# A neighbour mask turned by VectorE instead of TensorE in a two-layer graph network

## The chip, the cores and the metric

One core of a Trainium2 chip runs the whole kernel. The metric is device time in microseconds (us) for one execution, the median of several. TensorE is the matrix engine, VectorE (DVE in the profile) and ScalarE (ACT) do elementwise work, GpSimd (POOL) does elementwise work and issues transfers, SyncE (SP) issues transfers. SBUF is the on-chip memory with 128 partitions, PSUM the memory into which TensorE writes[...].

## What is computed

128 graphs of 128 nodes with 256 features each pass through two layers. The change is in layer 0, in its message passing between neighbours:

```python
h = jnp.maximum(_layernorm(x, axis=-1), 0.0)
s = h @ w_se.T + b_se                          # three features for each node
sq = jnp.sum(s * s, axis=-1)
dist = sq[:, :, None] + sq[:, None, :] - 2.0 * jnp.einsum('bnd,bmd->bnm', s, s)
A = jnp.exp(-dist) * mask                      # mask is adj, (128, 128, 128) of 0 and 1
msg = jax.nn.relu(h @ w_msg.T + b_msg)
x_nmp = jnp.einsum('bnm,bmd->bnd', A, msg)
```

The other parts of layer 0 are two convolutions along the nodes (one of width 17, computed here by a Fourier transform) and a gated unit which takes the convolution's result, `x_nmp` and `h`. Layer 1 works on 25 nodes of each graph alone. All data are float32.

## The kernel before

Graphs are worked on in 32 groups of four (`GB = 4`, `NQ = 32`). Four stages follow one another on TensorE. `stage_a(q)` normalizes a group, turns it, stores it transposed in DRAM (`hTd[q]`), and applies the first convolution and the Fourier transform. `stage_b(bat)` multiplies the 40 frequencies of half of all graphs. Both run twice, for groups 0 to 15 and for 16 to 31: a, b, a, b. Then `stage_c(q)` does the gated unit, and `block(blk)` the second layer beside it.

The message passing is in `early(q)`, once for each group, and runs beside the stages as a filler. Its body is the generator `neighbours` (L608 to L660). The loads for it are issued one group ahead by `load_n(q)` (L571): the transposed features `hT` (512 KB) and the adjacency `ad` (256 KB), both on SyncE's queue, into buffers of which there are two each. The queue also carries stage_b's weights (`wf`, L512) and stage_a's input (`xa`, L381), in program order.

`neighbours` computes, in this order, with a `yield` after each step:

1. `pse` (L614), the node features, and `ef` and `lr`, the factors of the distance (L618, L621);
2. the messages for two graphs and then for the other two: `pm` (L630), evacuated to `msg` by VectorE (L633) and ScalarE (L635);
3. the attention: `pds[j]` (L643) gets the exponent of graph j; `adj` of graph j is transposed by TensorE into the other half of the same PSUM tile (L645); ScalarE takes the exponential into `aT[:, j]` (L647); VectorE multiplies `aT[:, j]` by the transposed adjacency out of PSUM (L648);
4. twice: `px` (L656), messages by attention, for two graphs, evacuated to `xnmp` (L658).

The attention is needed with the sending node on the partitions, which is why the adjacency has to be turned.

The order of all instructions is fixed when the program is built. Each generator yields two numbers: the time that its step takes on TensorE, and a delay before which its next step isn't due. `Order.run` (L183) keeps a clock, takes of the lanes whose next step is due the one with the least work done in proportion to its weight, and lets it emit its next step. The engines then run their instruction streams in that order, each in its own, waiting on semaphores. Lane `beside` holds `early`; its weight is 0.66 and 0.2 beside the two runs of stage_a, 0.5 and 0.65 beside those of stage_b, and 0.5 afterwards.

In stage_b one frequency is a product `pa` of two factors and a product `pb` of their sums (L526). GpSimd forms the sums in SBUF one frequency ahead (`xs`, L520, and the third slot of `wf`, L521). ScalarE copies `pb` to `kk` (L557), and VectorE forms `y` from `pa` and `kk` (L558), which GpSimd's queue stores (L562). During the second stage_a GpSimd also folds the gate weights (`fold_gates`, L326).

PSUM is divided into three buffers `gat` and five buffers `tmp`, a bank each; `pds` takes four of `tmp` and each is free again after the last reader of it. The pool `fr`, which holds `ef`, `lr`, `msg`, `aT`, has one buffer for each name.

Of the kernel before, what the change touches and what calls it, by code (L numbers as in the profile page):

```python
# [9 lines left out]
FP = mybir.dt.float32  # L10
AF = mybir.ActivationFunctionType
# [4 lines left out]
B, N, D = 128, 128, 256  # L16
# [3 lines left out]
P = 128  # L20
GB = 4
# [20 lines left out]
WIDE = 32  # L42
# [165 lines left out]
def kernel(ctx: ExitStack, tc: tile.TileContext, x, adj, consts, vecs, w_se, conv1_w,  # L208
                    conv2_w, w_msg, b_msg, w_ih, w_hh, W1, W2, b2, fusion_w, out):
    nc = tc.nc  # L210
# [7 lines left out]
    ptmp = ctx.enter_context(tc.tile_pool(name="ptmp", bufs=5, space=PSUM))  # L218
# [14 lines left out]
    def c(name):  # L233
        a, b = CAT[name]
        return cst[:, a:b]
# [5 lines left out]
    ident = c("ident")  # L241
# [127 lines left out]
    LATE, XA, MOM = {}, {}, {}  # L369
# [201 lines left out]
    def load_n(q):  # L571
        hT = LATE["io"].tile([P, 2, 512], FP, tag="hT", name=f"hT{q}")
        nc.sync.dma_start(out=hT, in_=hTd[q])
        ad = LATE["io"].tile([P, GB, N], FP, tag="adj", name=f"adj{q}")
        nc.sync.dma_start(out=ad, in_=adj[q * GB:(q + 1) * GB].rearrange("b n m -> n b m"))
        return hT, ad

    SUMS = {}
# [29 lines left out]
    def neighbours(q, hT, ad, xm):  # L608


        pse = ptmp.tile([P, 512], FP, tag="tmp", name=f"pse{q}")
        for k in range(2):
            for j in range(GB):
                nc.tensor.matmul(pse[j * WIDE:(j + 1) * WIDE, :N], wse9[:, k],  # L614
                                 hT[:, k, j * N:(j + 1) * N], start=(k == 0), stop=(k == 1))
        ef = LATE["fr"].tile([P, 4, N], FP, tag="ef", name=f"ef{q}")
        for i in range(4):
            nc.scalar.activation(ef[:, i], pse[:, :N], AF.Identity, scale=emb[:, i:i + 1],  # L618
                                 bias=embb[:, i:i + 1])
        lr = LATE["fr"].tile([P, 2, N], FP, tag="lr", name=f"lr{q}")  # L620
        nc.vector.tensor_tensor(lr, ef[:, 0::2], ef[:, 1::2], ALU.mult)  # L621
        yield 0.5, 0.0

        msgs = []
        for h in range(2):
            pm = ptmp.tile([P, 2, D], FP, tag="tmp", name=f"pm{q}_{h}")
            for i in range(2):
                j = 2 * h + i
                for k in range(2):
                    nc.tensor.matmul(pm[:, i], hT[:, k, j * N:(j + 1) * N], LATE["wmsg"][:, k],  # L630
                                     start=(k == 0), stop=(k == 1))
            msg = LATE["fr"].tile([P, 2, D], FP, tag=f"msg{h}", name=f"msg{q}_{h}")
            nc.vector.tensor_tensor(  # L633
                msg, pm, LATE["bmsg"][:, None, :].to_broadcast([P, 2, D]), ALU.add)
            nc.scalar.activation(msg, msg, AF.Relu)  # L635
            msgs.append(msg)
            yield 1.75, 0.0

        pds = [ptmp.tile([P, 2, N], FP, tag="tmp", name=f"pd{q}_{j}") for j in range(GB)]
        aT = LATE["fr"].tile([P, GB, N], FP, tag="aT", name=f"aT{q}")  # L640
        for j in range(GB):
            rows = slice(j * WIDE, (j + 1) * WIDE)
            nc.tensor.matmul(pds[j][:, 0], lr[rows, 0], lr[rows, 1], start=True, stop=True)  # L643
        for j in range(GB):
            nc.tensor.transpose(pds[j][:, 1], ad[:, j], ident)  # L645
        for j in range(GB):
            nc.scalar.activation(aT[:, j], pds[j][:, 0], AF.Exp)  # L647
            nc.vector.tensor_mul(aT[:, j], aT[:, j], pds[j][:, 1])  # L648
        yield 0.9, 3.0


        for h in range(2):
            px = ptmp.tile([P, 2, 2, N], FP, tag="tmp", name=f"px{q}_{h}")
            for i in range(2):
                for dc in range(2):
                    nc.tensor.matmul(px[:, dc, i], msgs[h][:, i, dc * P:(dc + 1) * P],  # L656
                                     aT[:, 2 * h + i], start=True, stop=True)
            nc.vector.tensor_copy(xm[:, :, h * 256:(h + 1) * 256],  # L658
                                  px.rearrange("p d i n -> p d (i n)"))
            yield 0.9, 0.0  # L660

    def early(q):

        while q not in A_DONE:
            yield 0.0, 0.5
        if q not in EN:
            EN[q] = load_n(q)
            yield 0.0, 6.0
        hT, ad = EN.pop(q)
        if q + 1 < NQ and q + 1 in A_DONE:  # L670
            EN[q + 1] = load_n(q + 1)
        xm = LATE["fr"].tile([P, 2, 512], FP, tag="xnmp", name=f"xnmp{q}", bufs=2)
        yield from neighbours(q, hT, ad, xm)
        nc.gpsimd.dma_start(out=xmd[q], in_=xm)
        E_DONE.add(q)
# [510 lines left out]
```

## Time and profile before

| | us |
|---|---|
| median of 3 runs | 2072.65 |
| lowest and highest of them | 2071.14, 2078.92 |
| span of the profiled execution | 2070.6 |
| TensorE busy (share of the span) | 2032.3 (98%) |
| VectorE busy | 1161.9 (56%) |
| GpSimd busy | 730.1 (35%) |
| ScalarE busy | 712.7 (34%) |

The span runs from the first instruction of the program to the last one in the profiled execution; the times of the runs also hold what lies around it. The granted TensorE clock was 0.993 over the span. By 40 slices of 51.8 us, the 16 DMA engines are busy for more than nine tenths up to 155 us (stage_a), for 0.74 to 0.90 of the time from 155 to 362 us (the first stage_b and the end of what lies before it), for 0.48 to 0.60 from 362 to 518 us, for 0.77 or 0.78 up to 673 us (the second stage_b), and for less than half of the time after that.

In the views below PE is TensorE's matmul, PEld its weight load, which overlaps it; a line such as L645 is the line of the kernel; `pd<-cst,adj` names what is written and read. TensorE's matmuls overlap each other as well, so that what one costs is read from the start of one group to the start of the next.

### The profile page before, as it was taken

The numbers are of one execution on the slowest core, as the hardware profiler recorded it, in microseconds if no ns is written. First come the engines' busy times: TensorE is split into PE (matmuls) and PEld (weight loads), VectorE is DVE, ScalarE is ACT, GpSimd is POOL, SyncE is SP. The second block draws the span as 40 slices with busy tenths as digits, with TensorE's granted clock in tenths as the row PEclk, the third lists the DMA queues.
The fourth block names the chain that finished last, engine by engine and source line by source line (L and its number), as shares of the span: only waits on it lengthen the run. The fifth ranks groups of instructions, "written<-read, shape, count | busy, mean of one in ns | idle before, by whom it ended". The sixth has DMA issues, their size and how long they took to land.

```text
span 2070.6 us, 31082 instructions
## 1 busy us (share of the span) xinstructions
PE 2032.3 (98%) x11316; PEld 1649.4 (80%) x11316; DVE 1161.9 (56%) x2711; ACT 712.7 (34%) x1611; POOL 730.1 (35%) x898
## 2 busy tenths in 40 slices
PE   7998999999999999999999999999999999999998
PEld 5667888888888788788778787878787888778875
DVE  6774445874433556646654654566456655654542
ACT  4663223444222444233222332232332323323333
POOL 3552665333664123322422243233223323233230
PEclk9999999999999999899999999999999999999999
DMA  9997788545777444223323232322232332323121
GB/s 215 294 284 237 259 273 269 180 153 202 254 257 249 142 125 139 75 75 90 85 62 90 84 83 76 106 79 75 82 93 72 81 96 80 86 77 102 35 74 52
DMA packets 190135, 281.72 MB, mean 136 GB/s; under 512 B 23625, under 2 KB 143374, under 8 KB 189982
## 3 DMA queue, kind: packets, MB, share of 16 engines
q1 hardware_dynamic: 156942, 185.46, 31.4%
q0 software_dynamic: 32656, 93.98, 14.3%
q8 instruction: 90, 1.47, 0.3%
q14 instruction: 63, 0.52, 0.1%
q10 hardware_dynamic: 384, 0.28, 0.1%
HBM read 187.34 MB, written 92.27 MB: 135 GB/s over the span
## 4 chain that ended last, share of the span: by engine, by line
PE 93%; DVE 2%; DMA 2%; POOL 1%; issue 1%; ACT 1%; SPq 0%; DVEq 0%; POOLq 0%; ACTq 0%
PE p L738 42%; PE pa L526 7%; PE pm L630 5%; PE ph L1044 5%; PE pz L1053 5%; PE pc L421 4%; PE pb L526 3%; PE pi L703 3%; PE pf L432 3%; PE px L656 3%; PE pg L1087 2%; PE po L884 1%; PE pc L717 1%; PE pw L474 1%; PE ph L410 1%; PE py L1027 1%
## 5 line engine op out<-in xcount | busy, mean ns | idle before, releaser
L864 POOL TENSOR_TENSOR d<-hTc,r 128x512 f32<-128x512 f32 x64 | 81.9, 1280 | 244.4 <-ACT r L861 233.8
L526 PE MATMUL pa<-wf,X 128*128 128x256 f32 x640 | 152.2, 381 | 0.0
L893 POOL DMA_DIRECT2D out<-xt x128 | 72.0, 569 | 214.5 <-DVE xt L890 211.6
L558 DVE SCALAR_TENSOR_TENSOR y<-pa,kk 128x512 f32<-128x512 f32 x78 | 53.8, 690 | 151.2 <-ACT kk L557 151.1
L753 ACT ACTIVATE z<-z,brz 128x256 f32<-128x256 f32 x128 | 58.1, 501 | 226.7 <-DVE z L810 192.9
L738 PE MATMUL p<-th,wrz 128*128 128x256 f32 x512 | 132.8, 382 | 0.0
L738 PE MATMUL p<-tm,wrz 128*128 128x256 f32 x512 | 132.3, 381 | 0.0
L738 PE MATMUL p<-tc,wrz 128*128 128x256 f32 x512 | 131.5, 379 | 0.0
L526 PEld LDWEIGHTS pa<-wf,X 128*128 128x128 f32 x640 | 118.1, 190 | 16.2 <-issue 2.0
L630 PE MATMUL pm<-wmsg,hT 128*128 128x256 f32 x512 | 123.5, 387 | 0.0
L421 PE MATMUL pc<-c1w,hTa 128*128 128x256 f32 x512 | 121.6, 384 | 1.2 <-ACT hTa L412 1.2
L720 DVE SCALAR_TENSOR_TENSOR xc<-pc,s_bn,hTc 128x256 f32<-128x256 f32 x128 | 53.1, 478 | 123.3 <-PE pc L717 123.3
L1046 ACT ACTIVATE hh<-ph,vec 128x96 f32<-128x96 f32 (+3 forms) x160 | 64.2, 402 | 136.6 <-PE ph L1044 127.0
L630 PEld LDWEIGHTS pm<-wmsg,hT 128*128 128x128 f32 x512 | 97.1, 193 | 16.0 <-ACT kk L557 1.4
L1044 PE MATMUL ph<-yz,w 128*128 128x96 f32 (+3 forms) x640 | 108.4, 322 | 1.0 <-issue 1.0
L421 PEld LDWEIGHTS pc<-c1w,hTa 128*128 128x128 f32 x512 | 94.5, 191 | 18.3 <-DVE h L424 4.8
L738 PEld LDWEIGHTS p<-tm,wrz 128*128 128x128 f32 x512 | 97.9, 191 | 13.5
L1053 PE MATMUL pz<-hh,w 128*128 128x96 f32 (+3 forms) x640 | 107.3, 321 | 0.0
L738 PEld LDWEIGHTS p<-th,wrz 128*128 128x128 f32 x512 | 94.9, 191 | 13.0 <-issue 0.8
L738 PEld LDWEIGHTS p<-tc,wrz 128*128 128x128 f32 x512 | 95.0, 190 | 12.1 <-issue 0.5
L738 PE MATMUL p<-hTc,wrz 128*128 128x256 f32 x384 | 102.9, 391 | 1.6 <-ACT u L772 1.6
L1044 PEld LDWEIGHTS ph<-yz,w 128*128 128x128 f32 x640 | 86.7, 190 | 21.0 <-issue 15.4
(202 smaller groups left out, 4557.1 us busy)
## 6 DMA issues: line engine op xcount, KB each, us to landing
wf<-wfd SPq DMA_DIRECT2D x160, 256.0 KB, 3.5
wfd<-ws POOLq DMA_DIRECT2D x64, 320.0 KB, 9.2
yd<-y POOLq DMA_DIRECT2D x80, 256.0 KB, 4.3
yt<-yd SPq DMA_DIRECT2D x64, 320.0 KB, 5.0
w<-in_W SPq DMA_DIRECT2D x40, 512.0 KB, 3.6
xa<-in_x SPq DMA_DIRECT2D x128, 128.0 KB, 5.5
hTd<-hTa POOLq DMA_DIRECT2D x32, 512.0 KB, 6.6
hT<-hTd SPq DMA_DIRECT2D x32, 512.0 KB, 6.2
```

The source lines that it names most:

```text
L421: nc.tensor.matmul(pc[:, i], hT[:, k, (2 * h + i) * N:(2 * h + i + 1) * N], c1w[:, k], start=(k == 0), stop=(k == 1))
L432: nc.tensor.matmul(pf[:, i, :F * NB], h1[:, 2 * h + i, k * P:(k + 1) * P], fwd, start=True, stop=True)
L526: nc.tensor.matmul(ps, xk(k), WF[f][:, k, s], start=(k == 0), stop=(k == 1))
L630: nc.tensor.matmul(pm[:, i], hT[:, k, j * N:(j + 1) * N], LATE["wmsg"][:, k], start=(k == 0), stop=(k == 1))
L656: nc.tensor.matmul(px[:, dc, i], msgs[h][:, i, dc * P:(dc + 1) * P], aT[:, 2 * h + i], start=True, stop=True)
L703: nc.tensor.matmul(pi[b * 64:(b + 1) * 64], inv[:F], yt[:, b::2], start=True, stop=True)
L738: nc.tensor.matmul(ps[:, m], w[:, i, k, m * P:(m + 1) * P], factor(i, x, t), start=first and j == 0, stop=last and j == len(n) - 1, skip_g ...
L864: nc.gpsimd.tensor_sub(d, hT[:, dc], r[:, dc])
L893: nc.gpsimd.dma_start(out=out[q * GB + j, WIDE:].rearrange("(t n) c -> n t c", n=WIDE), in_=xt[j * WIDE:(j + 1) * WIDE, 1:4])
L1044: nc.tensor.matmul(ph, w1[:, k, m * P:(m + 1) * P], yz[:, k, :, o:o + n], start=(k == 0), stop=(k == 1))
L1046: nc.scalar.activation(hh[:, m], ph, AF.Relu, bias=v("b1", g * 4 + m))
L1053: nc.tensor.matmul(pz, w2[:, g, m, cc * P:(cc + 1) * P], hs[g][:, m], start=(m == 0), stop=(m == 3))
```

## The change

The adjacency is loaded by four DMAs in place of one. DMA w writes partitions 32w to 32w+31 and takes columns 32w to 32w+31 of the adjacency, in contiguous runs of 32 elements (128 B) where before a run was a row of 128 (512 B). In the tile, each block of 32x32 then stands where the transposed matrix has it, itself not yet turned. One VectorE transpose of the whole tile (128x512), which turns each block of 32x32 by itself, makes the transposed adjacency `adT` in SBUF. TensorE's four transposes and their half of the `pds` tiles are gone. The product with the mask is made for two graphs at a time, in SBUF. The step's declared TensorE time goes from 0.9 to 0.45.

```diff
@@ load_n
-        ad = LATE["io"].tile([P, GB, N], FP, tag="adj", name=f"adj{q}")
-        nc.sync.dma_start(out=ad, in_=adj[q * GB:(q + 1) * GB].rearrange("b n m -> n b m"))
+        ad = LATE["io"].tile([P, GB * 4, WIDE], FP, tag="adj", name=f"adj{q}")
+        for w in range(4):
+            nc.sync.dma_start(out=ad[w * WIDE:(w + 1) * WIDE],
+                              in_=adj[q * GB:(q + 1) * GB, :, w * WIDE:(w + 1) * WIDE]
+                              .rearrange("b (k n) m -> n (b k) m", n=WIDE))
@@ neighbours
-        pds = [ptmp.tile([P, 2, N], FP, tag="tmp", name=f"pd{q}_{j}") for j in range(GB)]
+        pds = [ptmp.tile([P, N], FP, tag="tmp", name=f"pd{q}_{j}") for j in range(GB)]
         aT = LATE["fr"].tile([P, GB, N], FP, tag="aT", name=f"aT{q}")
+        adT = LATE["fr"].tile([P, GB, N], FP, tag="adT", name=f"adT{q}")
+        nc.vector.transpose(adT.rearrange("p b n -> p (b n)"),
+                            ad.rearrange("p b n -> p (b n)"))
         for j in range(GB):
             rows = slice(j * WIDE, (j + 1) * WIDE)
-            nc.tensor.matmul(pds[j][:, 0], lr[rows, 0], lr[rows, 1], start=True, stop=True)
+            nc.tensor.matmul(pds[j], lr[rows, 0], lr[rows, 1], start=True, stop=True)
         for j in range(GB):
-            nc.tensor.transpose(pds[j][:, 1], ad[:, j], ident)
-        for j in range(GB):
-            nc.scalar.activation(aT[:, j], pds[j][:, 0], AF.Exp)
-            nc.vector.tensor_mul(aT[:, j], aT[:, j], pds[j][:, 1])
-        yield 0.9, 3.0
+            nc.scalar.activation(aT[:, j], pds[j], AF.Exp)
+            if j % 2:
+                nc.vector.tensor_mul(aT[:, j - 1:j + 1], aT[:, j - 1:j + 1], adT[:, j - 1:j + 1])
+        yield 0.45, 3.0
```

## The prediction

> **What bounds the kernel now.** I read the page first, then the chain of waits inside the stretch that the change touches, then the adjacency tile's own view, and last the timeline of one turn of the helper `neighbours`.
>
> The page, busy shares and chain by line (whole span):
>
> ```profile
> PE 2032.3 (98%) x11316; PEld 1649.4 (80%) x11316; DVE 1161.9 (56%) x2711; ACT 712.7 (34%) x1611; POOL 730.1 (35%) x898
> ...
> PE 93%; DVE 2%; DMA 2%; POOL 1%; issue 1%; ACT 1%; SPq 0%; DVEq 0%; POOLq 0%; ACTq 0%
> ```
>
> TensorE is the end-setting engine: 93% of the chain that ended last is its work. So an instruction that leaves TensorE is worth its time, unless another engine then arrives late.
>
> The instructions of the adjacency tile and of the tile it is multiplied into:
>
> ```profile
> L645 PEld LDWEIGHTS pd<-cst,adj x128: 137/141/143, 174.9 to 803.9; 128*128 128x128 f32 x128
> L645 PE MATMUL pd<-cst,adj x128: 272/273/329, 174.9 to 804.0; 128*128 128x128 f32 x128
> L575 SPq DMA_DIRECT2D adj<-in_adj x32: 373/432/911, 164.6 to 769.0; - x32
> ...
> L647 ACT ACTIVATE aT<-pd x128: 257/278/299, 175.9 to 805.5; 128x128 f32<-128x128 f32 x128
> L648 DVE TENSOR_TENSOR aT<-aT,pd x128: 277/280/289, 176.1 to 805.9; 128x128 f32<-128x128 f32 x128
> ```
>
> Everything happens between 164 and 806 us. A transpose is 273 ns from start to end, but they overlap; what four cost TensorE must be read in order of time. One turn in the frequency products (stage_b), timeline 254.5 to 258.5 us (start, length, engine, line):
>
> ```profile
> 254.73 0.50 PE L643 MATMUL pd<-lr 32*128 32x128 f32 x8
> ...
> 254.96 0.72 POOL L520 TENSOR_TENSOR xs<-X 128x256 f32<-128x256 f32 x1 [1.86 <-PE pb L526]
> 255.17 0.42 PEld L645 LDWEIGHTS pd<-cst,adj 128*128 128x128 f32 x4
> ...
> 255.32 0.69 DVE L558 SCALAR_TENSOR_TENSOR y<-pa,kk 128x512 f32<-128x512 f32 x1 [2.37 <-ACT kk L557]
> 255.53 0.79 ACT L647 ACTIVATE aT<-pd 128x128 f32<-128x128 f32 x4 [0.25 <-PE pd L645]
> 255.55 1.60 PEld L526 LDWEIGHTS pa<-wf,X 128*128 128x128 f32 x8
> 255.65 1.26 POOL L521 TENSOR_TENSOR wf<-wf 128x512 f32<-128x512 f32 x1
> ...
> 255.93 0.87 DVE L648 TENSOR_TENSOR aT<-aT,pd 128x128 f32<-128x128 f32 x4
> ...
> 258.25 0.50 PE L656 MATMUL px<-aT,msg 128*128 128x128 f32 x3
> ```
>
> The four transposes begin at 255.17 and the next product's weights follow at about 255.55 to 255.6: 0.42 us of TensorE. ScalarE's exponentials start only after them, VectorE's product ends at 256.80, and its reader px starts at 258.25: 1.45 us of slack. The turn before this one began at 234.75, so a turn takes 19.98 us, all of it TensorE's.
>
> How long VectorE takes when both operands lie in SBUF, in the same turns (L621: minimum, median, maximum):
>
> ```profile
> L621 DVE TENSOR_TENSOR lr<-ef x32: 417/426/3478, 170.5 to 797.4; 128x256 f32<-128x256 f32 x32
> ```
>
> Mostly 426 ns, at times 2.34 us (as at 244.99, while POOL ran xs and wf one behind the other), at most 3.48.
>
> [...] Today's L648 has a PSUM operand and never exceeds 289 ns; the changed product has both operands in SBUF. [...] The packet records here show 27 ns for 512 B and 13 ns for the 100 B pieces of the `aj` loads, so bytes get dearer by far, a piece does not.
>
> **The change part by part.**
>
> *Removed, TensorE:* 128 transposes, 0.42 us for each four, 32 turns: 13.4 us. From the first transpose to the next matmul of another line it is 0.49 us in nearly every turn; the upper bound is 15.8, and I take 13.4[...].
>
> *Removed, waiting:* a `pd` bank is now free when ScalarE has read it, not when VectorE has multiplied. TensorE's waits on L648 that are not px's own are 0.9 (ph) and 0.8 us (pf); I count 1.0 of 1.7. Also ScalarE's 5.7 us of waits on L645 go, but ScalarE is no bound: nothing.
>
> *Added, VectorE:* one transpose of 128x512. No row shows it. The nearest is a 128x512 copy or sum, 690 ns (L558, L633)[...]. Taken 0.69 us, upper end 1.4[...], lower end 0.3. Four products of 280 ns become two of 128x256: 0.42 each undisturbed. So VectorE goes from 1.12 to 1.53 us a turn, +13 us in 1162: it stays far from the bound.
>
> *Is the product still in time?* Count from pd's start (254.73). y holds VectorE until 1.28; the transpose then runs to 2.00; the first product of two graphs meets POOL's wf, which ends at 2.18. The blocked L621 cases end 0.86 us after the POOL instruction does (247.33 against 246.46), so the first pair is ready at 3.04, unblocked at 2.42. px starts at 3.52 now and 3.10 without the transposes. It just fits; with the transpose at 1.4 us POOL is done when the product comes, and 2.7 + 0.4 = 3.1 fits as well. The second pair (3.5) is wanted 0.9 us after px's start. Behind the product on VectorE stands the next y, wanted at about 3.77. Cost: nothing in the 15 turns of the products; if the cover goes, 0.1 to 1.9 us a turn (rival 1).
>
> *Where there is no cover:* in turns 1 and 25 px follows pd at once and TensorE already waits 0.97 us for aT. There removing the transposes gains nothing and the longer VectorE part adds about 0.3: 2 x (0.42 + 0.3) = 1.4 us lost. In the five turns of stage_a between 353 and 480 us POOL runs weight folding with instructions of 1.8 us (L326), and VectorE is 82% busy (42.58 of 51.70 us): I charge 0.4 us each, 2.0; ends 0 and 8 us.
>
> *Loads:* 32 adjacency DMAs become 128, 512 pieces of 512 B a turn become 2048 of 128 B. At 13 to 15 ns a piece over 16 engines it is 1.8 us a turn in place of 0.86; in a turn of 20 us with the engines 0.78 to 0.90 busy, +5 points. Adjacency is issued 17 to 60 us before use and its last piece lands within 7 us nearly always, so VectorE will not wait for it. On SyncE's queue three more issues of 0.43 us stand before the next wf load; in the turn at 259.91 that load is not issued until 261.97, since it waits for pb's buffer. wf lands 2.35 us or more before POOL reads it where a landing is recorded, mostly 3.5 and more even just behind an adjacency load. Taken as nothing; bounds 0 and 6 us.
>
> *Order:* the step's declared cost falls from 0.9 to 0.45 us, so the planner interleaves a little differently from the first turn on. That moves work without adding any: 0, give or take 4 us.
>
> Sum: -13.4 - 1.0 + 1.4 + 2.0 = -11.0 us. Profiled span 2070.6 becomes 2059.6. The median shown, 2072.65, lies 2.05 above the span (what surrounds it and the spread of runs); with it 2061.6.
>
> **Rivals.**
>
> 1. *Slower: the product on VectorE comes late[...].* If it finds POOL at the start of xs rather than the end of wf, as L621 does at 244.99, it takes 2.34 us; with the transpose at 1.4 the first pair is ready at 1.28 + 1.4 + 2.34 = 5.0, px waits 1.9 us in 15 turns, 29 us, and 2061.6 + 29 = 2090. With the short transpose the wait is 1.2, and 2080. From 0.73 us of waiting a turn on (the first pair later than 3.8 us after pd) the gain is gone. For it: L621's record in these very turns. Against: POOL's start is tied to pb, and at pd it is in the middle of its pair.
> 2. *No change: the time is handed to other engines.* In stage_a VectorE is nearly full, and evacuations that come later stop TensorE. It needs to give back 5 us or more over the 17 turns outside the products, 0.3 us each or more: 2067. For it: TensorE idles 3.0 us between 362 and 466 us already. Against: 98% busy, and VectorE at 40 to 60% elsewhere.
> 3. *The small pieces are slow:* at 27 ns each the adjacency takes 3.5 us of all engines a turn, 2.6 more, still inside wf's slack of 3.5: 2063. From about 40 ns on POOL's sum waits and pb with it; at 50 ns it is 6.4 us, 5.5 more, 2.0 beyond the slack, in 15 turns 30 us: 2091.
>
> **How the numbers follow.** Forecast 0.50, rival 2 0.28, rival 1 0.17, rival 3 as a loss 0.05. What a measurement of this kernel can tell from no change is about 0.5%, 10 us; the runs shown differ by nearly 8. The likeliest case, 2061.6 rounded to 2061.5, lies at 0.54%, close to that line. Its own range is 2054 to 2067 (transposes at 15.8, order ±4, loads 0 to 6). To hold 8 in 10 the range takes in rival 2 and the short form of rival 1: 2054 to 2081. Faster 0.49, same 0.30, slower 0.21.
>
> **What would show it.** Right: no matmul reads adj; pd's weights are followed by the next product within about 0.45 us; the turn of 19.98 us shrinks by 0.4; the transpose row at about 0.7 us x32; px has no wait above 0.2 us in the products. Wrong: px waiting for aT in most turns, product rows on VectorE with a mean near 1 us or more, POOL's xs or wf longer, pa or pb waiting for wf, or VectorE waiting for an adjacency DMA.

## The result, and the profile after

| | before | changed |
|---|---|---|
| median of 20 runs each, us | 2074.56 | 2081.69 |
| lowest and highest, us | 2071.14, 2082.31 | 2074.49, 2088.47 |
| span of the profiled execution, us | 2070.6 | 2076.7 |

The ratio of changed to before is 1.003, with a 95% interval of 1.0018 to 1.0043: the changed kernel is slower, by 4 to 9 us. The forecast was 11 us less. In the terms of the prediction the change lies within 0.5%, on the slow side, and the median is just above the upper end of the range (2081).

The page of the changed kernel, busy shares and chain by engine:

```profile
PE 2024.0 (97%) x11188; PEld 1638.8 (79%) x11188; DVE 1165.9 (56%) x2679; ACT 700.3 (34%) x1603; POOL 729.0 (35%) x898
...
PE 94%; DVE 2%; DMA 1%; issue 1%; SPq 1%; ACT 1%; POOL 1%; DVEq 0%; ACTq 0%; POOLq 0%
```

TensorE has 128 matmuls fewer and 8 us less busy time, as the change intends, and still the kernel ends later. So TensorE must stand idle more. The view of the tile that the transpose writes (minimum, median, maximum of a duration in ns, then who waited for it, us and times):

```profile
L653 DVE TENSOR_TENSOR aT<-aT,adT x64: 410/424/2703, 178.0 to 750.5; 128x256 f32<-128x256 f32 x64
L645 DVE STREAM_TRANSPOSE adT<-adj x32: 694/702/705, 176.9 to 748.3; 128x512 f32<-128x512 f32 x32
...
who waited for it (us, times):
  PEld px L661: 11.1, 5
  PE px L661: 9.9, 5
```

The new operations take what was forecast, 0.70 and 0.42 us. But px waits for them 9.9 us in all, five times. One ordinary turn of the first stage_b, timeline 231.3 to 235.6 us:

```profile
231.58 0.50 PE L649 MATMUL pd<-lr 32*128 32x128 f32 x8
...
232.02 1.99 PE L526 MATMUL pa<-wf,X 128*128 128x256 f32 x8
...
232.50 1.27 POOL L521 TENSOR_TENSOR wf<-wf 128x512 f32<-128x512 f32 x1
232.78 0.70 DVE L645 STREAM_TRANSPOSE adT<-adj 128x512 f32<-128x512 f32 x1
233.58 0.81 DVE L653 TENSOR_TENSOR aT<-aT,adT 128x256 f32<-128x256 f32 x2
...
234.71 1.05 PE L661 MATMUL px<-aT,msg 128*128 128x128 f32 x8
```

Here all is as the prediction has it: the next product follows pd after 0.44 us, both products with the mask are ready 2.81 us after pd, and px starts at 3.13 without a wait. The loss isn't in these turns. TensorE's longest waits, of the kernel before and then of the changed one (who waited for whom: us in total, times, longest). A wait of 10 us at the start of the program, which both have, is left out:

```profile
...
PE pse L614 <- DMA hT<-hTd: 6.6, 1, 6.6
PE p L738 <- DVE r L854: 2.8, 2, 2.5
PE px L656 <- DVE aT L648: 2.3, 3, 1.0
```

```profile
...
PE px L661 <- DVE aT L653: 9.9, 5, 3.7
PE pse L617 <- DMA hT<-hTd: 8.0, 1, 8.0
PE p L743 <- DVE r L859: 4.9, 4, 2.2
PE pd L649 <- ACT hTa L412: 3.1, 5, 0.6
PE ph L410 <- DVE h L424: 2.5, 1, 2.5
```

Three of the five in the second list have nothing to do with the adjacency: `r`, `hTa` and `h` belong to stage_c and stage_a. That points at what stands next to what. And the two kernels do differ in their order. TensorE's stream in a turn of the first stage_b, of the kernel before (258 to 262.5 us) and of the changed one (234 to 240 us):

```profile
258.25 1.05 PE L656 MATMUL px<-aT,msg 128*128 128x128 f32 x8
259.14 1.89 PE L526 MATMUL pa<-wf,X 128*128 128x256 f32 x8
260.87 1.03 PE L526 MATMUL pb<-wf,xs 128*128 128x256 f32 x4
261.74 0.94 PE L656 MATMUL px<-aT,msg 128*128 128x128 f32 x7
```

```profile
234.71 1.95 PE L661 MATMUL px<-aT,msg 128*128 128x128 f32 x16
236.50 1.89 PE L526 MATMUL pa<-wf,X 128*128 128x256 f32 x8
```

The two halves of px stood on either side of a frequency product and now follow each other directly. So a turn has four frequency products in place of five, and is 17.00 us long (231.58 to 248.59) where it was 19.98. The message passing thus runs ahead. Its last px comes at 754 us, before at 809; when the first gate product of stage_c starts, pd is still to come for one group, before for five.

Where the idle time arises shows best if the span from the first frequency product to the end is split. In this table the columns from "first b" to "later" are time without a matmul up to the last matmul, by stage, and "idle, sum" is their total. "Layer 1 is under way" is taken as 20 us after its first `py` product. "Clock" is an estimate of what the clock cost: half of the time for which the profile has TensorE at half clock. "Rest" is what remains, in the main TensorE's own work; it holds the 6 us after the last matmul too, and is low by up to 1.4 us where idle time at half clock is counted twice. All in us, worked out from the trace. Each row is from one profiled execution, whose time lies up to 6 us from the median of its kernel's runs:

| kernel | length | first b | second a | second b | c, until layer 1 is under way | later | idle, sum | clock | rest |
|---|---|---|---|---|---|---|---|---|---|
| before | 1878.1 | 0.0 | 3.6 | 0.0 | 4.8 | 3.4 | 11.9 | 10.2 | 1856.0 |
| changed | 1880.9 | 2.6 | 6.4 | 0.0 | 10.4 | 4.1 | 23.5 | 12.1 | 1845.3 |
| e1_cost_09 | 1867.5 | 0.0 | 3.4 | 0.0 | 7.2 | 3.4 | 14.1 | 8.5 | 1844.9 |
| e2_before_045 | 1888.4 | 0.0 | 5.9 | 0.0 | 8.5 | 4.0 | 18.4 | 12.2 | 1857.7 |
| e3_one_load | 1867.0 | 0.0 | 3.4 | 0.0 | 7.2 | 3.4 | 14.0 | 8.4 | 1844.5 |
| e4_psum_exp | 1885.1 | 0.0 | 10.9 | 0.0 | 9.7 | 2.4 | 23.0 | 15.4 | 1846.8 |
| e5_cost_moved | 1878.2 | 0.0 | 6.5 | 0.0 | 8.3 | 3.6 | 18.4 | 13.6 | 1846.1 |
| e6_turn_early | 1866.2 | 0.3 | 2.5 | 0.0 | 7.2 | 3.4 | 13.4 | 8.3 | 1844.5 |
| e7_no_mask | 1864.8 | 0.0 | 2.5 | 0.0 | 5.2 | 3.4 | 11.1 | 10.3 | 1843.4 |
| e8_early_045 | 1883.8 | 0.5 | 6.5 | 0.4 | 11.3 | 4.1 | 22.8 | 15.6 | 1845.5 |
| e9_px_apart | 1876.4 | 1.7 | 3.2 | 0.0 | 9.8 | 3.4 | 18.1 | 12.1 | 1846.3 |
| e10_both | 1873.9 | 0.0 | 2.2 | 0.0 | 9.3 | 3.4 | 14.9 | 12.5 | 1846.5 |

TensorE was spared 10.7 us of work (1856.0 to 1845.3) and lost 11.6 to idling and 1.9 to the clock, 2.8 us in all. The medians are 7 us apart: the changed kernel's profiled execution also reached the first frequency product 3.2 us later (195.7 against 192.5 us), and was itself 3.3 us faster than the median of its runs. The rows of the experiments are read below.

### The profile page after: what moved, and what is told of

Read it like the earlier page. It is cut to its first block, busy times and chain, and to the rows that moved or that the text cites. A ratio compares the mean times of both kernels' runs of the same rounds, so it can differ in the third digit from the quotient of the medians.

```text
span 2076.7 us, 30941 instructions
## 1 busy us (share of the span) xinstructions
PE 2024.0 (97%) x11188; PEld 1638.8 (79%) x11188; DVE 1165.9 (56%) x2679; ACT 700.3 (34%) x1603; POOL 729.0 (35%) x898
## 4 chain that ended last, share of the span: by engine, by line
PE 94%; DVE 2%; DMA 1%; issue 1%; SPq 1%; ACT 1%; POOL 1%; DVEq 0%; ACTq 0%; POOLq 0%
PE p L743 42%; PE pa L526 7%; PE pm L633 5%; PE ph L1049 5%; PE pz L1058 5%; PE pc L421 5%; PE pf L432 3%; PE pb L526 3%; PE pi L708 3%; PE px L661 3%; PE pw L474 2%; PE pg L1092 2%; PE po L889 1%; PE ph L410 1%; PE pc L722 1%; PE py L1032 1%
## 5 line engine op out<-in xcount | busy, mean ns | idle before, releaser
L743 PEld LDWEIGHTS p<-tm,wrz 128*128 128x128 f32 x512 | 97.9, 191 | 13.5
L743 PEld LDWEIGHTS p<-tc,wrz 128*128 128x128 f32 x512 | 95.0, 190 | 12.1 <-issue 0.5
```

The costliest lines, as they stand in the source:

```text
L743: nc.tensor.matmul(ps[:, m], w[:, i, k, m * P:(m + 1) * P], factor(i, x, t), start=first and j == 0, stop=last and j == len(n) - 1, skip_g ...
```

## The experiments

The theory after the result: the transposes brought what was forecast, and the new order of instructions, which follows from the declared 0.45, gave more than that back (order theory). Rivals: VectorE's longer part costs it in every order (latency theory; in its sharper form, the GpSimd theory, a VectorE product with two SBUF operands is held up by GpSimd's sums, as `lr` took 2.34 us beside such sums at 244.99 us of the kernel before, where its median is 0.43), and the loads in small pieces do.

**The order of before, with the change; and the order of the change, without it.**

```diff
 e1_cost_09, against the changed kernel
-        yield 0.45, 3.0
+        yield 0.9, 3.0
 e2_before_045, against the kernel before
-        yield 0.9, 3.0
+        yield 0.45, 3.0
```

> The changed kernel with the step's declared cost back at 0.9, so that every instruction is emitted in the order of the kernel before; only the transposes, the load and the product differ from it. Order theory (the loss comes from the different interleaving, which puts turns of the message passing where nothing covers them): 9 to 13 us faster than before, 2061 to 2066, ratio 0.994 to 0.996; turns of 19.55 us in the first run of stage_b; TensorE's waits for aT at most 5 us in all. Latency theory (the longer VectorE part[...] cost it wherever the turns stand): within 4 us of the changed kernel, ratio above 1.000, waits for aT near 10 us again.

> The kernel before with the declared cost at 0.45 and nothing else: TensorE still turns the adjacency, in the order of instructions of the changed kernel. Order theory: slower than before by 10 to 19 us, ratio 1.005 to 1.009, since it has the new order's gaps and still the 13 us of transposes. Latency theory: within 4 us of before, ratio 0.998 to 1.002.

Measured: e1 2067.59 us, ratio 0.9962 (0.9951 to 0.9972). e2 2085.18 us, ratio 1.0056 (1.0038 to 1.0075). With the old order, the change makes the kernel faster; the new order alone makes it slower. In the table, e1's length is 10.6 us below before and e2's 10.3 above. The same edit of one declared number, with the change made, is worth 13.4 us (1880.9 less 1867.5). The other way round, the change of the operations is worth 10.6 us in the old order and 7.5 in the new one (1888.4 less 1880.9). e1's waits behind the start are nearly back to before's, but for px:

```profile
...
PE px L661 <- DVE aT L653: 4.7, 3, 1.9
PE p L743 <- DVE r L859: 3.3, 2, 2.5
PE p L743 <- ACT u L777: 1.6, 1, 1.6
```

The order theory stands, and the latency theory's main claim falls. By the ratio e1 gains a little less than forecast, 8 us in place of 9 to 13. Its profiled execution reached the first frequency product 11.6 us later than before's did (204.1 against 192.5 us), after a wait of 5.2 us in the first stage_a, where neither the order nor an operation differs. In the twelve traces the first frequency product comes anywhere from 192.5 to 204.1 us, at 193.5 and 199.9 in e3 and e6, which are emitted in much the same order as e1. The table therefore begins behind the start.

**The load as before.** The mask's blocks are misplaced, else as e1.

```diff
 e3_one_load, against e1_cost_09
-        for w in range(4):
-            nc.sync.dma_start(out=ad[w * WIDE:(w + 1) * WIDE],
...
+        nc.sync.dma_start(out=ad, in_=adj[q * GB:(q + 1) * GB].rearrange("b n m -> n b m"))
```

> As e1_cost_09, but the adjacency comes in one DMA of 512 B pieces as before; the blocks of the mask then stand in the wrong places, so the mask applied is another one. Load theory (the 128 B pieces and the three more issues cost time on the queue): at least 5 us faster than e1_cost_09. Order theory and latency theory: within 3 us of e1_cost_09.

Measured: 2063.96 us, ratio 0.9951 (0.9932 to 0.9970), an interval that overlaps e1's; 1867.0 against 1867.5 us in the table. By the table the load theory falls; the medians are 3.6 us apart, which by itself is within the noise. The changed kernel's packet records fit: a 128 B piece takes 13.5 ns in the mean, half of the 28 ns of a 512 B piece, and the last one lands within 10 us of the first issue where the transpose comes 12 us or more behind it.

**One operand in PSUM.** This takes the second SBUF operand away from the product.

```diff
 e4_psum_exp, against the changed kernel
-            nc.scalar.activation(aT[:, j], pds[j], AF.Exp)
-            if j % 2:
-                nc.vector.tensor_mul(aT[:, j - 1:j + 1], aT[:, j - 1:j + 1], adT[:, j - 1:j + 1])
+            nc.scalar.activation(pds[j], pds[j], AF.Exp)
+            nc.vector.tensor_mul(aT[:, j], pds[j], adT[:, j])
```

> The changed kernel with the exponential written in place in PSUM and four products of 128x128 that read it there, so that no product has two operands in SBUF. [...] (products blocked by GpSimd are a good part of the loss): the wait of TensorE at turn 11 (2.6 us near 355 us) is gone, no product above 0.35 us, and the time falls by 3 us or more against the changed kernel, ratio to before at most 1.002. Order theory: the blocked turn goes, but turns 1, 29 and 30 still wait (7 us in all), and the time stays within 4 us of the changed kernel, ratio 1.001 to 1.003.

Measured: 2085.51 us, ratio 1.0049 (1.0028 to 1.0071); the interval overlaps the changed kernel's. The 2.6 us of idle time at turn 11 are gone (0.0 in the first stage_b by the table), but not the loss:

```profile
...
PE px L660 <- DVE aT L652: 6.7, 3, 3.5
PE p L742 <- DVE r L858: 4.8, 4, 2.2
PE pf L432 <- DVE aT L652: 4.3, 6, 0.9
```

The third line is new: the banks of pd are held until VectorE has multiplied, and stage_a's `pf` waits for them. In the second stage_a e4 idles 10.9 us, the changed kernel 6.4. The early release of the banks alone is not shown to be worth that: e2, in the same order, holds the banks until VectorE has multiplied too and idles 5.9 there. The edit thus takes one wait away and brings another, so its time doesn't decide about the GpSimd theory. The table does: without the long products of turn 11 TensorE is spared the 2.6 us of the first stage_b, and the waits at turns 1, 29 and 30 stay (6.7 us). So the GpSimd theory, whose forecast the expectation gives first, falls as the main explanation. The order theory's range for e4 (1.001 to 1.003) was missed as well, by the new wait.

At turn 11 of the changed kernel (turns are counted from 0), where the first stage_b ends, two products last long (timeline 346 to 359 us):

```profile
351.23 1.03 POOL L273 TENSOR_TENSOR rs<-rs,cst 128x4 f32<-128x4 f32 x1 [2.77 <-DVE rs L272]
...
352.60 4.96 DVE L653 TENSOR_TENSOR aT<-aT,adT 128x256 f32<-128x256 f32 x2
...
352.86 0.74 POOL L520 TENSOR_TENSOR xs<-X 128x256 f32<-128x256 f32 x1
...
353.54 1.27 POOL L521 TENSOR_TENSOR wf<-wf 128x512 f32<-128x512 f32 x1
...
355.32 0.74 POOL L520 TENSOR_TENSOR xs<-X 128x256 f32<-128x256 f32 x1
...
355.36 1.16 PE L661 MATMUL px<-aT,msg 128*128 128x128 f32 x8 [1.47 <-DVE aT L653]
```

Both products begin just ahead of a pair of GpSimd's sums (352.60 against 352.86, 355.23 against 355.32), and they take 2.70 and 2.34 us, as `lr` with its two SBUF operands did before (2.34 us). VectorE is on time here: its product begins 2.00 us after pd (350.60), as in the other turns of the first stage_b. It is GpSimd that is late. Its `xs` begins 2.26 us after pd and not 0.23, behind a step of stage_a's statistics (L273) that waited for VectorE, and the issue of a store. It cost TensorE 2.6 us, once. That the meeting with GpSimd is what prolongs the products is read from the times and not tested further.

**The price of the transposes alone.** The mask is left out altogether.

```diff
 e7_no_mask, against the kernel before
-            nc.tensor.transpose(pds[j][:, 1], ad[:, j], ident)
-        for j in range(GB):
...
-            nc.vector.tensor_mul(aT[:, j], aT[:, j], pds[j][:, 1])
```

> The kernel before without the four transposes and without the product with the mask; the attention is the exponential alone, and the adjacency is loaded but not read. The order of what is left is that of the kernel before. It prices what TensorE's transposes cost: if 13.4 us, as predicted, the ratio is 0.993 to 0.9945 and the stretch from the first frequency product to the end is 13 to 15 us shorter than before; if the pipeline keeps part of it, 9 to 12 us. What e1_cost_09 lies above it is the price of all that VectorE and the load got: 0 to 4 us.

Measured: 2060.72 us, ratio 0.9925 (0.9909 to 0.9942), a little below the forecast; 13.3 us less than before in the table. Of these 12.6 are TensorE's own work, 0.42 us for each of the 30 turns behind the table's start, as the prediction has it; the rest is less waiting, and e7 lacks the product with the mask too. e1 lies 2.7 us above: the price of all that VectorE and the load took over.

**The transpose two steps earlier.**

```diff
 e6_turn_early, against e1_cost_09; e8_early_045 is the same against the changed kernel
         nc.vector.tensor_tensor(lr, ef[:, 0::2], ef[:, 1::2], ALU.mult)
+        adT = LATE["fr"].tile([P, GB, N], FP, tag="adT", name=f"adT{q}")
+        nc.vector.transpose(adT.rearrange("p b n -> p (b n)"),
+                            ad.rearrange("p b n -> p (b n)"))
         yield 0.5, 0.0
...
-        adT = LATE["fr"].tile([P, GB, N], FP, tag="adT", name=f"adT{q}")
-        nc.vector.transpose(adT.rearrange("p b n -> p (b n)"),
-                            ad.rearrange("p b n -> p (b n)"))
```

> As e1_cost_09, with VectorE's transpose emitted two steps earlier, behind lr, where VectorE waits for ScalarE anyway. If the transpose's place is what makes the uncovered turns wait: TensorE's wait for aT at turns 1 and 25 falls from 1.86 us to about 1, the sum over all turns from 4.7 to 3 us or less, and the time is 1 to 3 us below e1_cost_09, ratio 0.994 to 0.996. If ScalarE's exponential and the product set that wait: no change from e1_cost_09 within 1 us.

> As e6_turn_early, with the declared cost at 0.45, which is the changed kernel with its transpose emitted earlier. Order theory: it stays slower than e1_cost_09 by 6 us or more, ratio 0.999 to 1.003, since the turns at the start of stage_c remain uncovered. Latency theory: the waits for aT (9.9 us in the changed kernel) fall below 5 us and the ratio to 0.998 or less.

Measured: e6 2062.52 us, ratio 0.9942 (0.9920 to 0.9963), the fastest kernel here that computes everything; e8 2081.39 us, ratio 1.0023 (1.0010 to 1.0036). e8 bears the order theory out: it is 16.3 us longer than e1 in the table, and px still waits 8.0 us for aT where the latency theory has less than 5. In e6 px's wait did not move: 4.7 us, three times, 1.86 at turn 1 as without the edit. One turn without cover, e6's timeline 188.5 to 193 us:

```profile
189.91 0.69 DVE L639 TENSOR_TENSOR msg<-pm,bmsg 128x512 f32<-128x512 f32 x1 [0.40 <-PE pm L636]
...
190.69 0.63 ACT L641 ACTIVATE msg<-msg 128x512 f32<-128x512 f32 x1 [0.46 <-DVE msg L639]
191.23 0.76 ACT L651 ACTIVATE aT<-pd 128x128 f32<-128x128 f32 x4
191.69 0.76 DVE L653 TENSOR_TENSOR aT<-aT,adT 128x256 f32<-128x256 f32 x2 [1.09 <-ACT aT L651]
...
192.17 1.23 PE L661 MATMUL px<-aT,msg 128*128 128x128 f32 x6 [1.86 <-DVE aT L653]
```

The chain is msg, its ReLU, two exponentials, the product of two graphs; VectorE stands idle for 1.09 us in front of that product. The transpose was never on it. Whether e6 is faster than e1 is open, since the intervals overlap; the table has 1.3 us between them.

**Which feature of the order?** Two simple ideas were tried: that the smaller declared sum gives the message passing more than its share, and that the loss is what is no longer there as cover when stage_c begins.

```diff
 e5_cost_moved, against the changed kernel (first step of neighbours)
-        yield 0.5, 0.0
+        yield 0.95, 0.0
 e9_px_apart, against the changed kernel; e10_both is the same against e8_early_045
             nc.vector.tensor_copy(xm[:, :, h * 256:(h + 1) * 256],
                                   px.rearrange("p d i n -> p d (i n)"))
-            yield 0.9, 0.0
+            yield 0.9, 1.0 if h == 0 else 0.0
```

> The changed kernel, with the 0.45 that the attention step's declared cost lost added to the first step of the same turn (0.5 to 0.95), so that a turn declares as much work as before while its own step declares what it takes. Share theory (the smaller declared sum lets the message passing run ahead of its share, with four products a turn in place of five, and so leaves turns uncovered): the turns of the first stage_b are near 19.6 us again, the last px comes near 805 us and not near 754, and the time is within 4 us of e1_cost_09, ratio 0.994 to 0.998. Rival (what matters is when px falls due after pd, not the share): turns of 17 us stay, ratio 1.001 or more.

> The changed kernel with one number added: a delay of 1.0 between the two halves of px, so that a frequency product comes between them again and a turn of the first stage_b has five products. The declared cost of the attention step stays at 0.45. Cover theory (the loss is that the turns run ahead, so that few are left when stage_c begins and nothing covers its first waits): about six turns are left when the first gate product starts, the last px comes after 780 us, TensorE idles 12 to 16 us from the first frequency product to the end in place of 23.5, and the ratio is 0.994 to 0.998. Rival (it is the declared cost as such, or one of the new interleavings is as good as another): ratio 1.000 to 1.004.

> As e9_px_apart, with VectorE's transpose emitted behind lr as in e6_turn_early. Cover theory: the ratio is 0.993 to 0.997, near e6_turn_early's 0.9942. Rival: 1.000 to 1.003, near e8_early_045's 1.0023.

Measured: e5 2071.51 us, ratio 0.9984 (0.9974 to 0.9995), e9 2071.55 us, 0.9986 (0.9976 to 0.9996), e10 2069.39 us, 0.9975 (0.9965 to 0.9985). By their ratios all three lie between the changed kernel and e1, and outside the ranges of both the theory and its rival. e5 keeps the turns of 17.0 us, with its last px at 760 us, so the share theory falls; yet it is faster than the changed kernel, so its rival doesn't hold either. e9 did put the order right by the measure of the cover theory: pd is still to come for five groups when the first gate product starts, the last px comes at 804 us, and the idle time of the first stage_b and of the second stage_a falls. But at the seam between stage_b and stage_c it loses nearly as much as the changed kernel (9.8 us against 10.4 in the table). There its timeline (668 to 690 us) has

```profile
673.93 0.50 PE L649 MATMUL pd<-lr 32*128 32x128 f32 x8
678.42 2.08 PE L661 MATMUL px<-aT,msg 128*128 128x128 f32 x8 [3.99 <-DVE aT L653]
```

a turn with nothing between pd and px. So a part of the loss is recovered in e9, and the number of turns left isn't the whole of it. What sets the rest in the changed kernel is to be seen at its own seam (timeline 703 to 723 us):

```profile
708.38 0.31 PEld L649 LDWEIGHTS pd<-lr 32*128 32x128 f32 x8 [0.33 <-issue]
...
710.34 0.68 DVE L636 TENSOR_TENSOR msg<-pm,bmsg 128x512 f32<-128x512 f32 x1
...
712.59 2.07 PE L661 MATMUL px<-aT,msg 128*128 128x128 f32 x8 [3.70 <-DVE aT L653]
```

VectorE runs eight subtractions for stage_c's first group (L589, from 707.41 to 710.42) before it evacuates the second half of this turn's messages, since the order put stage_c's step between the two; px waits 3.70 us behind them. From 711.0 us on, within that wait, the profile has the clock at half for 10.2 us.

## Why the prediction was wrong

It was wrong in one step, and nearly right in the others.

- *Removed, TensorE, 13.4 us:* right in size. The table has 30 of the 32 turns; in e7 TensorE's own work there is 12.6 us less, and in e1 11.1. What the 1.5 between them are stays open.
- *Removed, waiting, 1.0 us:* not found. The waits of `pf` and `ph` for the banks are gone in e1, but others of the same size stand in their place, and the second stage_a idles 3.4 us in place of 3.6.
- *VectorE, +13 us:* too little. It is busy 1183.7 us in e1, 21.8 more than before. The prediction took the four old products at 280 ns each, 1.12 us, where its own timeline has 0.87 for the four together; the two new ones take 0.81. TensorE lost nothing by it in the turns of stage_b: the first pair is ready 2.47 us after pd, where the prediction feared 3.04.
- *The turns of stage_b:* right. They shrink from 19.98 to 19.59 us in e1, px doesn't wait in them, the transpose takes 0.70 us, and the product mostly 0.42. The 0.69 us forecast for the transpose were those of rows of the same shape (690 ns), its ends of 0.3 and 1.4 the author's estimate. (Before, 18 turns have a frequency product between pd and px, where the prediction counts 15; this bears on its rivals' sums alone.)
- *No cover at turns 1 and 25:* right. px's wait there grows from 0.97 to 1.86 us; 0.72 each was charged, 0.89 came. Turn 28, which was not charged, goes from 0.31 to 1.01 as well.
- *GpSimd's weight folding in stage_a, 2.0 us:* too much. The second stage_a idles 3.4 us in e1 and 3.6 before.
- *Loads, nothing:* right, by e3.
- *The sum, -11.0 us:* that of e1 with the order kept: -10.6 in the stretch behind the start, -8 (5.8 to 10.2 by the interval) over whole runs. That it fits so well is in part luck: the 10.6 are made of 11.1 less work, 2.2 more idling and 1.7 less at half clock, and the prediction has no term for the clock.
- *"Order: ... That moves work without adding any: 0, give or take 4 us":* this is the step that failed. It is +10.3 us on the kernel before (e2), and +13.4 us on the changed one (e1 against it). The sentence is true of the work: TensorE's own share is the same to 2 us in either order. The term was put at nothing because no work is added, and the waits that the order decides were not counted. A step declared half a microsecond shorter lets the filler run ahead, and after 32 turns its last px comes 55 us earlier. Between before and e2 TensorE idles 6.5 us more and loses 2.0 more to the clock; between e1 and the changed kernel it is 9.4 and 3.6. This lies in the second stage_a, at the start of stage_c and, in the changed kernel, at turn 11.

Of the rivals, the second was nearest in size: the time went back to waits outside the products, in stage_a and at the start of stage_c. But its cause, VectorE nearly full, doesn't fit: VectorE is busier in e1 (1183.7 us) than in the slower changed kernel (1165.9). It was seen to come late at turn 30 alone, by what the order had put in front. The first, the product held up beside GpSimd, decided one turn of 32 (2.6 us at turn 11); why GpSimd's sums should prolong it was not shown.

What stays open: which rule tells a good order from a bad one. Neither the declared sum (e5) nor the number of turns left for stage_c (e9) does by itself. That the order costs the time is shown by e1 and e2; how it does so was shown for waits in single turns only.

## What to carry to other kernels

When the emission order is computed from declared costs, an edit of a cost is a change of its own, to be measured apart: apply the real edit with the old costs first, then the costs alone. A saving on the engine that sets the end can be lost when the order of the work around it moves along. After such a change, look at the seams between stages for new waits, not only at the turns that were edited.

## What was not expected of the hardware

In the changed kernel the profile has TensorE at half clock for 10.2 us from 711.0 us on, 2.1 us into its wait of 3.70 us. e9 has 13.7 us from 676.3, 1.9 us into its wait of 3.99, and the kernel before has 10.2 us from 845.3, 1.5 us into a wait of 2.48 us for stage_c's `r`. That the waits bring the half clock was not tested, and not every stretch has one: the changed kernel is also at half clock for 3.4 us from 1670.2, where TensorE doesn't stop. In the table the clock's loss goes from 8.5 us (e1) to 12.2 (e2) between the two orders.

Whether the product is held up seems to depend on where in GpSimd's pair of sums it begins. In turns of stage_b it starts 1.08 us after GpSimd's second sum (233.58 against 232.50), 0.19 us before that sum ends, and takes 0.41 to 0.47 us; at turn 11 it starts 0.26 us ahead of the first sum, and two products take 4.96 us. For the product this is rare, but for `lr` (L621 before, L624 in the changed kernel), which has two SBUF operands as well, it isn't: it takes over 0.5 us in 12 of 32 turns before, in nearly every turn of the first stage_b, and in 4 of the changed kernel. No engine waits for `lr` in the kernel before.
